# Narrow heads' scores as a pair, two engines on the queries' banks, and a rearranged start and end of a latent attention stage

## The chip, the core and the metric

The kernel runs on one core of a Trainium2 chip. The core has a matrix engine (TensorE, PE in the profile; its weight loads are a row of their own, PEld), a vector engine (VectorE, DVE), a scalar engine (ScalarE, ACT), a general engine (GpSimd, POOL) and a queue engine for transfers (SyncE, SP). Each engine works through its own instructions in order and waits for others through semaphores. Matmul results land in PSUM, which holds eight banks of 512 float32 numbers per partition; everything else stands in SBUF, which has 128 partitions. The metric is the device time of one execution in microseconds (us); lower is better.

## The reference

Two transformer layers run on x of shape (2, 1024, 256), float32. Each adds an attention and a feed-forward part to x, both computed from the same normalized x. The change lies in the attention of the second layer, a latent attention with 16 heads. The lines that matter:

```python
q = rmsnorm(hidden_states @ wq_a.T, q_a_ln_w) @ wq_b.T
q_nope, q_pe = (q[..., :NOPE], q[..., NOPE:])
ckv = hidden_states @ wkv_a.T
kv = rmsnorm(ckv[..., :KV_LORA], kv_a_ln_w)
k_pe = ckv[..., KV_LORA:][:, None, :, :]
q_pe = apply_rope(q_pe, cos, sin)
k_pe = apply_rope(k_pe, cos, sin)
q_abs = jnp.einsum('bhsd,hdc->bhsc', q_nope, q_absorb)
scores = (jnp.einsum('bhsc,btc->bhst', q_abs, kv) + jnp.einsum('bhsd,bxtd->bhst', q_pe, k_pe)) * SCALE
scores = jnp.where(causal, scores, jnp.finfo(scores.dtype).min)
attn = jax.nn.softmax(scores, axis=-1)
x = jnp.einsum('bhst,btc->bhsc', attn, kv)
x = jnp.einsum('bhsc,hdc->bhsd', x, out_absorb)
return x.transpose(0, 2, 1, 3).reshape(b, s, NH * VH) @ wo.T
```

Keys and values are the same 64 latent numbers per token, shared by all heads; a query has those 64 (the latent part) and 64 rotated ones. The mask is causal, so a block of 128 query tokens needs only the keys up to its own end.

## The kernel before

Everything up to 769 us of the span (the first layer, the second layer's feed-forward, keys, folded weights) is untouched. The stage of the change is the second layer's attention, from about 770 us to the end. Its order of work is written out by hand (`manual_schedule`): the engines take instructions in the order of the program text, and the framework adds the semaphore waits from the order in which tiles are written and read.

**Steps.** There are 16 steps: two batches, four pairs of query blocks (i, 7 - i), and two groups `g` of eight heads. The wide block i has 1024, 896, 768 or 640 keys, the narrow one 128, 256, 384 or 512. Each step has four cycles (c = 0 to 3); a cycle takes two heads of the wide block and two of the narrow one.

**Scores (`scores`, L1046 to L1069).** A head's scores are matmuls of up to 512 keys into a pair of PSUM banks (L1059; each float32 matmul shows as two passes in the profile), then DVE masks them, writes them negated to SBUF and takes the row's minimum (L1064, with a small read of the accumulator), then ACT takes the exponential and the row sum (L1067). A wide head takes a whole pair of banks. The two narrow heads share a pair, one bank each; the second stands in the program behind the first one's maximum and exponential. `turn_over` (L1073) transposes the weights in 32 by 32 blocks on DVE at the end of the cycle.

**Banks.** Pairs of banks (`pair`, tag "s") exist twice. Scores, projected queries, the transposed reciprocals and the output use them in turn. The other four banks hold the value products of one step (`ps_o`).

**What else a cycle holds.** While step s has its scores taken, the step before (`prev`) gets a quarter of its value products in each cycle (`product`, L1107: 72 small matmuls, 144 passes) and the step before that (`older`) is finished: `normalize` (L1117, DVE) at c = 0, `output` (L1130) at c = 1, `add` (L1142) at c = 2, and with it the transfer out for the second group. `inverse` (L1078 on DVE, L1081 on POOL) makes the reciprocals of the row sums of `prev` at c = 0, and `inverse_T` (L1092, and copies by ACT at L1098) transposes them at c = 3.

**Queries of the next step.** At c = 0 and c = 2 a block's queries are projected (`Query.project`, L994 and L1001): one bank holds the part to rotate, the other the latent part of both halves of the heads. In `rotate`, ACT copies the first bank to `t1` (L1018), then the latent parts (L1008, two copies of 64 partitions), then two halves of `t1`, swapped, to `t2` (L1022). POOL multiplies by cosine and sine (L1023, L1024) and adds into `qc` (L1028, four adds of 32 partitions). For the very first step the two projections and rotations stand ahead of all cycles; there DVE multiplies, DVE and POOL add, and both queries use the one `t1` and the one `t2`.

**The end.** After the last step with scores comes one pass of one cycle with all 36 blocks of value products of the last step in a row, then the output of the step before it, then the reciprocals; then a last pass normalizes, multiplies out, adds and stores.

Of the kernel before, what the change touches and what calls it, by code (L numbers as in the profile page):

```python
# [17 lines left out]
F32 = mybir.dt.float32  # L18
# [5 lines left out]
P = 128  # L24
# [4 lines left out]
SC = 512  # L29
# [17 lines left out]
def two_layers(ctx: ExitStack, tc: tile.TileContext, a: dict, out: bass.AP):  # L47
# [56 lines left out]
    with ExitStack() as scope:  # L104
# [233 lines left out]
        def scores(g, n, pair):  # L338
            iq, j = WEIGHTS[n]
            k, q = heads[g, 1], heads[g, 0]  # L340
            w = WIDTH[n]
            at = (4 * iq + 4) * P - w
            if (g, n) not in held:
                held[g, n] = l0t.tile([P, 4, SC], F32, tag="p", name="p", bufs=3)
            p = held[g, n]
            t = ps_pair()
            for c in pair:
                nc.tensor.matmul(  # L348
                    t[:, c % 2, :w], quad(k, c, D0 + 1)[:, j * P : (j + 1) * P],
                    quad(q, c, D0 + 1)[:, at : at + w],  # L350
                    start=True, stop=True, tile_position=(32 * c, 0),
                )

            def weights():
                nc.scalar.activation(p[:, pair[0] : pair[0] + 2, :w], t[:, :, :w], AF.Exp)  # L355
                if j >= 4 * iq:

                    nc.gpsimd.affine_select(  # L358
                        out=p[:, pair[0] : pair[0] + 2, :P], in_=p[:, pair[0] : pair[0] + 2, :P],
                        compare_op=ALU.is_ge, fill=0.0, base=0,  # L360
                        pattern=[[0, 2], [1, P]], channel_multiplier=-1,
                    )

            return weights
# [589 lines left out]
    with ExitStack() as scope:  # L954
# [8 lines left out]
        def pair(name):  # L963
            return ps.tile([P, 2, SC], F32, tag="s", name=f"ps_{name}", bufs=2)
# [6 lines left out]
        class Query:  # L971
# [33 lines left out]

            def latent(self):
                for hh in range(2):
                    nc.scalar.copy(  # L1008
                        self.qc[0:64, hh].rearrange("p r t -> p (r t)"),
                        self.lat[64 * hh : 64 * hh + 64],  # L1010
                    )

            def rotate(self, ahead=False):

                one, two = (nc.vector, nc.gpsimd) if ahead else (nc.gpsimd, nc.gpsimd)
                cos, sin = (t.unsqueeze(1).to_broadcast([P, QP, P]) for t in self.trig)
                t1 = att.tile([P, QP, P], F32, tag="t1", name="t1")
                nc.scalar.copy(t1.rearrange("p r t -> p (r t)"), self.pe)  # L1018
                self.latent()
                t2 = att.tile([P, QP, P], F32, tag="t2", name="t2")  # L1020
                for lo, hi in ((0, 64), (64, 0)):
                    nc.scalar.copy(t2[lo : lo + 64], t1[hi : hi + 64])  # L1022
                one.tensor_tensor(t1, t1, cos, ALU.mult)  # L1023
                one.tensor_tensor(t2, t2, sin, ALU.mult)  # L1024
                for hh in range(2):
                    for x in range(2):
                        at = 64 * x + 32 * hh
                        (one, two)[x].tensor_tensor(  # L1028
                            self.qc[64 + 32 * x : 96 + 32 * x, hh], t1[at : at + 32],
                            t2[at : at + 32], ALU.add,  # L1030
                        )
# [11 lines left out]
            s.p, s.q = {}, ready[b, i, g]  # L1043
            return s

        def scores(s, k, h):  # L1046

            w = P * (s.blocks[k] + 1)
            lo = 0
            if k == 0 or h % 2 == 0:  # L1050
                s.sc = pair("s").rearrange("p k c -> p (k c)")
                s.pp = att.tile([P, S], F32, tag="p", name="p", bufs=3)
            else:
                lo = SC
            sc, p = s.sc[:, lo : lo + w], s.pp[:, lo : lo + w]
            s.p[k, h] = p
            for n0 in range(0, w, SC):
                n1 = min(n0 + SC, w)
                nc.tensor.matmul(  # L1059
                    sc[:, n0:n1], s.q[k].qc[:, h // QP, h % QP, :],  # L1060
                    kT[:, s.b * S + n0 : s.b * S + n1], start=True, stop=True,
                )
            nmax = small.tile([P, 1], F32, tag="nmax", name="nmax")
            nc.vector.tensor_tensor_reduce(  # L1064
                p, sc, maskw[:, S - w :], -1.0, 3.0e38, ALU.add, ALU.min, nmax
            )
            nc.scalar.activation(  # L1067
                p, p, AF.Exp, bias=nmax, scale=-1.0, accum_out=s.rsum[:, k, h : h + 1]
            )  # L1069

        def turn_over(s, k, h):
            at = slice(0, s.nsb) if k == 0 else slice(s.nsb, NSB)
            nc.vector.transpose(s.pT[:, at, h, :], s.p[k, h])  # L1073

        def inverse(s):

            rinv = att.tile([P, 2, NH2], F32, tag="rinv", name="rinv", bufs=2)
            nc.vector.reciprocal(rinv, s.rsum)  # L1078
            s.rb = att.tile([P, 2, QP, 2, 64], F32, tag="rb", name="rb")
            for k in range(2):  # L1080
                nc.gpsimd.tensor_copy(  # L1081
                    s.rb[:, k],
                    rinv[:, k].rearrange("p (h r) -> p r h", h=2).unsqueeze(3).to_broadcast(
                        [P, QP, 2, 64]
                    ),
                )
# [27 lines left out]
        def normalize(s, k):  # L1114
            if k == 0:
                s.xT = att.tile([P, 2, QP, P], F32, tag="xT", name="xT")
            nc.vector.tensor_tensor(  # L1117
                s.xT[:, k].rearrange("p r (c y) -> p r c y", c=4),
                s.o[:, :, k * P : (k + 1) * P].rearrange("p c (r y) -> p r c y", r=QP),
                s.rT[:, k].rearrange("p (r c y) -> p r c y", r=QP, c=4), ALU.mult,  # L1120
            )
# [28 lines left out]
        with tc.manual_schedule():  # L1150
            steps = [(b, i, g) for b in range(B) for i in range(TB - 1, TB // 2 - 1, -1) for g in range(2)]
            ready = {}

            def ahead(step):

                b, i, g = step
                known = (b, i) == steps[0][:2]
                ready[step] = [
                    Query(b, t, g, k if known else None) for k, t in enumerate((i, TB - 1 - i))
                ]  # L1160
                return ready[step]

            for q in ahead(steps[0]):
                q.project()
                q.rotate(ahead=True)

            prev, older = None, None
            for at in range(len(steps) + 2):
                s = new_step(*steps[at]) if at < len(steps) else None
                nxt = ahead(steps[at + 1]) if at + 1 < len(steps) else ()  # L1170
                cycles = NCY if s is not None else 1
                for c in range(cycles):
                    heads = [] if s is None else [(k, 2 * c + h) for k in range(2) for h in range(2)]
                    if c == 0 and older is not None:
                        normalize(older, 0)
                        fetch_x(older)
                    if c == 2 and older is not None:
                        add(older)
                    for k, h in heads[:1]:
                        scores(s, k, h)  # L1180
                    if c == 0 and older is not None:
                        normalize(older, 1)
                    for k, h in heads[1:]:
                        scores(s, k, h)
                    if prev is not None:
                        for sb in range(c * NSB // cycles, (c + 1) * NSB // cycles):
                            product(prev, sb)
                    q = nxt[c // 2] if nxt and c % 2 == 0 else None
                    if q is not None:
                        q.project()  # L1190
                    if c == min(1, cycles - 1) and older is not None:
                        output(older)
                    if prev is not None:
                        if c == 0:
                            inverse(prev)
                        if c == cycles - 1:
                            inverse_T(prev)
                    for k, h in heads:
                        turn_over(s, k, h)
                    if q is not None:  # L1200
                        q.rotate()
                if s is None and older is not None:
                    add(older)
                older, prev = prev, s

# [66 lines left out]
```

## Time and profile before

| what | value |
|---|---|
| times of three runs, us | 1471.72, 1478.02, 1473.11 (median 1473.11) |
| the profiled execution | 1475.92 us, span 1474.2 us, mean granted TensorE clock 0.956 |
| busy in 811.4 to 1446.3 us of the span (634.9 us) | PE 556.2, DVE 374.6, ACT 302.3, POOL 237.5 us |
| granted clock there | 1.00 |
| idle before PE's score matmuls (L1059) from 778 us on | 84.3 us, of which 68.1 end with a maximum (nmax, L1064) |
| one value product run of a cycle (144 passes) | 2.32 us |

How to read the profile. A line of the timeline gives the start and the length in us, the engine, the line of the program, the operation, what is written and read, the shape, and how many instructions are merged; in brackets stands how long the engine was idle before and what ended that. A line of the waits gives who waited for whom, the total in us, how often, and the longest. A line of the windows gives the length of a stretch, then each engine's busy time and count, the granted clock as a share, the share of the DMA engines and their GB/s. Ends of matmuls are modelled, and consecutive matmuls overlap: the next starts before the last one's modelled end.

### The profile page before, as it was taken

The numbers are of one execution on the slowest core, as the hardware profiler recorded it, in microseconds if no ns is written. First come the engines' busy times: TensorE is split into PE (matmuls) and PEld (weight loads), VectorE is DVE, ScalarE is ACT, GpSimd is POOL, SyncE is SP. The second block draws the span as 40 slices with busy tenths as digits, with TensorE's granted clock in tenths as the row PEclk, the third lists the DMA queues.
The fourth block names the chain that finished last, engine by engine and source line by source line (L and its number), as shares of the span: only waits on it lengthen the run. The fifth ranks groups of instructions, "written<-read, shape, count | busy, mean of one in ns | idle before, by whom it ended". The sixth has DMA issues, their size and how long they took to land.

```text
span 1474.2 us, 36254 instructions
## 1 busy us (share of the span) xinstructions
PE 1317.6 (89%) x15614; PEld 781.1 (53%) x15614; DVE 770.3 (52%) x1893; ACT 671.6 (46%) x1250; POOL 460.4 (31%) x494
## 2 busy tenths in 40 slices
PE   6689999899999989998997888888888888888986
PEld 2233346264563543555774566565665656666655
DVE  3775544545456553124336656565556565655662
ACT  1224573453637546553315545445444454444441
POOL 2233333342414221003213444244334433443320
PEclk9659999899999999999997999999999999999999
DMA  4212301010101000001233000000000000000000
GB/s 179 74 31 56 101 8 23 0 23 1 22 1 22 23 1 18 15 1 54 59 95 58 5 17 6 24 10 23 10 12 17 6 27 6 24 9 15 11 17 10
DMA packets 61007, 41.09 MB, mean 28 GB/s; under 512 B 37648, under 2 KB 56848, under 8 KB 60592
## 3 DMA queue, kind: packets, MB, share of 16 engines
q1 hardware_dynamic: 60000, 35.51, 9.0%
q8 instruction: 122, 2.00, 0.6%
q0 software_dynamic: 416, 2.49, 0.4%
q10 hardware_dynamic: 432, 0.79, 0.2%
q14 instruction: 37, 0.30, 0.1%
HBM read 26.18 MB, written 10.49 MB: 25 GB/s over the span
## 4 chain that ended last, share of the span: by engine, by line
PE 77%; DVE 11%; ACT 5%; issue 4%; POOL 2%; DMA 1%; SPq 0%; ACTq 0%; DVEq 0%; POOLq 0%
PE ps_s L1059 12%; PE ps_m L307 11%; PE ps_o L1107 10%; DVE p L1064 6%; PE ps_m L558 5%; PE ps_o L373 5%; PE ps_m L461 4%; PE ps_m L430 4%; PE ps_t L1001 4%; PE ps_t L1130 4%; PE ps_m L228 4%; PE ps_t L994 2%; PE ps_m L573 2%; ACT qc L1008 2%; ACT t L1018 1%
## 5 line engine op out<-in xcount | busy, mean ns | idle before, releaser
L1059 PE MATMUL ps_s<-kT,qc 128*128 128x512 f32 (+3 forms) x768 | 290.7, 506 | 84.3 <-DVE nmax L1064 68.1
L1064 DVE CUSTOM_DVE_ANT_0 p<-ps_s,wpe 128x128 f32<-128x128 f32 (+7 forms) x256 | 189.7, 756 | 217.2 <-PE ps_s L1059 216.7
L1067 ACT ACTIVATE p<-p,nmax 128x128 f32<-128x128 f32 (+7 forms) x256 | 197.1, 770 | 187.4 <-DVE nmax L1064 186.1
L1059 PEld LDWEIGHTS ps_s<-kT,qc 128*128 128x128 f32 x768 | 129.8, 191 | 221.7 <-DVE nmax L1064 98.2
L355 ACT ACTIVATE p<-ps_s 128x1024 f32<-128x1024 f32 (+1 forms) x192 | 152.6, 808 | 167.1 <-PE ps_s L348 162.1
L307 PE MATMUL ps_m<-head,head 16*128 16x512 f32 (+3 forms) x672 | 193.7, 552 | 20.1 <-DVE nmx L318 14.0
L1073 DVE STREAM_TRANSPOSE pT<-p 128x128 f32<-128x128 f32 (+7 forms) x256 | 175.3, 742 | 0.0
L348 PE MATMUL ps_s<-head,head 17*128 17x512 f32 (+3 forms) x768 | 172.2, 553 | 0.0
L1028 POOL TENSOR_TENSOR qc<-t,t 32x512 f32<-32x512 f32 x124 | 158.8, 1280 | 34.9 <-issue 22.2
L1107 PE MATMUL ps_o<-pT,vrep 32*64 32x128 f32 x9216 | 152.1, 275 | 7.6 <-issue 5.3
L1107 PEld LDWEIGHTS ps_o<-pT,vrep 32*64 32x64 f32 x9216 | 135.5, 131 | 37.4 <-issue 35.9
L307 PEld LDWEIGHTS ps_m<-head,head 16*128 16x128 f32 x672 | 71.8, 189 | 119.7 <-DVE nmx L318 38.6
L1023 POOL TENSOR_TENSOR t<-t,cosq 128x512 f32<-128x512 f32 x28 | 35.7, 1274 | 293.9 <-issue 203.3
L358 POOL TENSOR_SCALAR_AFFINE_SELECT p<-p 128x256 f32<-128x256 f32 x128 | 51.5, 408 | 242.2 <-ACT p L355 241.0
L323 DVE TENSOR_REDUCE nmx<-ps_m 128x1 f32<-128x512 f32 x112 | 72.2, 686 | 44.0 <-PE ps_s L348 35.3
L558 PE MATMUL ps_m<-xnT,w 128*128 128x512 f32 x192 | 94.4, 620 | 0.0
L318 DVE CUSTOM_DVE_ANT_0 junk<-ps_m,maskz,nmx 128x512 f32<-128x512 f32 (+3 forms) x112 | 57.7, 548 | 59.2 <-PE ps_s L348 40.8
L1018 ACT COPY t<-ps_t 128x512 f32<-128x512 f32 x32 | 18.8, 586 | 146.5 <-PE ps_t L1001 126.0
L373 PE MATMUL ps_o<-p,v 128*32 128x512 f32 (+3 forms) x768 | 82.3, 501 | 0.0
L461 PEld LDWEIGHTS ps_m<-wpr,hT 128*128 128x128 f32 x512 | 62.3, 199 | 17.7 <-issue 6.6
L430 PE MATMUL ps_m<-xnT,wfc 128*128 128x512 f32 x128 | 68.6, 661 | 0.2
L461 PE MATMUL ps_m<-wpr,hT 128*128 128x128 f32 x512 | 68.5, 289 | 0.0
(175 smaller groups left out, 1786.7 us busy)
## 6 DMA issues: line engine op xcount, KB each, us to landing
rows<-proj SPq DMA_DIRECT2D x12, 512.0 KB, 2.6
stage<-rows SPq DMA_DIRECT2D x96, 64.0 KB, 3.1
w<-in_w SPq DMA_DIRECT2D x3, 768.0 KB, 4.7
x_sb<-in_x SPq DMA_DIRECT2D x4, 512.0 KB, 12.4
x<-x_sb SPq DMA_DIRECT2D x4, 512.0 KB, 3.2
fold_wo<-in_wo SPq DMA_DIRECT2D x8, 256.0 KB, 3.2
vrep<-kv SPq DMA_DIRECT2D x32, 64.0 KB, 2.1
xin<-x SPq DMA_DIRECT2D x16, 128.0 KB, 2.2
```

What stands on the lines that cost most here:

```text
L307: nc.tensor.matmul(t[:, :w], quad(q, c, D0)[:, i * P : (i + 1) * P], quad(k, c, D0)[:, k0 : k0 + w], start=True, stop=True, tile_position= ...
L348: nc.tensor.matmul(t[:, c % 2, :w], quad(k, c, D0 + 1)[:, j * P : (j + 1) * P], quad(q, c, D0 + 1)[:, at : at + w], start=True, stop=True, ...
L355: nc.scalar.activation(p[:, pair[0] : pair[0] + 2, :w], t[:, :, :w], AF.Exp)
L373: nc.tensor.matmul(quad(box["o"], c)[:, SC - w :], values[g][:, j, 32 * c : 32 * c + 32], p[:, c, :w], start=(j == 0), stop=(j == 4 * iq + ...
L461: nc.tensor.matmul(po[:, :P], f["h", hc // 2][:, hc % 2, t * P : (t + 1) * P], wpr[:, hc, cols], start=(hc == 0), stop=(hc == NH0 - 1),)
L558: nc.tensor.matmul(pw, w1t[f"w{i + 1}"][:, kc, hc * P : (hc + 1) * P], xnT1[n // 2][:, kc, (n % 2) * SC : (n % 2 + 1) * SC], start=(kc == ...
L1028: (one, two)[x].tensor_tensor(self.qc[64 + 32 * x : 96 + 32 * x, hh], t1[at : at + 32], t2[at : at + 32], ALU.add,)
L1059: nc.tensor.matmul(sc[:, n0:n1], s.q[k].qc[:, h // QP, h % QP, :], kT[:, s.b * S + n0 : s.b * S + n1], start=True, stop=True,)
L1064: nc.vector.tensor_tensor_reduce(p, sc, maskw[:, S - w :], -1.0, 3.0e38, ALU.add, ALU.min, nmax)
L1067: nc.scalar.activation(p, p, AF.Exp, bias=nmax, scale=-1.0, accum_out=s.rsum[:, k, h : h + 1])
L1073: nc.vector.transpose(s.pT[:, at, h, :], s.p[k, h])
L1107: nc.tensor.matmul(s.o[64 * hh : 64 * hh + 64, c, k * P : (k + 1) * P], vrep[32 * c : 32 * c + 32, s.b * 32 + sb, :], s.pT[32 * c : 32 * c ...
```

## The change

Four things move.

- `scores` takes a list of heads. For the narrow block it gets both heads of the cycle: their matmuls come first, then for each head the maximum and the exponential.
- In `rotate` the latent part is copied by DVE instead of ACT.
- The first step's two rotations get tiles of their own (two halves of a tile with the tag "p", of which there are three). The first is done by DVE alone; in the second POOL multiplies and adds the odd quarters, DVE adds the even ones. `rotate` takes the three engines as an argument.
- The pass after the last step has four cycles like the others: the value products come in quarters, the output of the step before stands after the second quarter, the transposed reciprocals after the third. `inverse` stands behind the first wide head of c = 0 instead of behind the projection.

```diff
             def latent(self):
                 for hh in range(2):
-                    nc.scalar.copy(
+                    nc.vector.tensor_copy(
                         self.qc[0:64, hh].rearrange("p r t -> p (r t)"),
                         self.lat[64 * hh : 64 * hh + 64],
                     )
...
-            def rotate(self, ahead=False):
-
-                one, two = (nc.vector, nc.gpsimd) if ahead else (nc.gpsimd, nc.gpsimd)
+            def rotate(self, engines=(nc.gpsimd, nc.gpsimd, nc.gpsimd), first=False):
+
+                one, even, odd = engines
...
-                t1 = att.tile([P, QP, P], F32, tag="t1", name="t1")
+                if first:
+                    t = att.tile([P, S], F32, tag="p", name="t12", bufs=3)
+                    t1, t2 = (
+                        t[:, SC * x : SC * x + SC].rearrange("p (r t) -> p r t", r=QP) for x in range(2)
+                    )
+                else:
+                    t1 = att.tile([P, QP, P], F32, tag="t1", name="t1")
+                    t2 = att.tile([P, QP, P], F32, tag="t2", name="t2")
...
-                        (one, two)[x].tensor_tensor(
+                        (even, odd)[x].tensor_tensor(
...
-        def scores(s, k, h):
+        def scores(s, k, hs):
...
+            sc = pair("s").rearrange("p k c -> p (k c)")
+            pp = att.tile([P, S], F32, tag="p", name="p", bufs=3)
+            for j, h in enumerate(hs):
+                for n0 in range(0, w, SC):
+                    n1 = min(n0 + SC, w)
+                    nc.tensor.matmul(
+                        sc[:, j * SC + n0 : j * SC + n1], s.q[k].qc[:, h // QP, h % QP, :],
+                        kT[:, s.b * S + n0 : s.b * S + n1], start=True, stop=True,
+                    )
+            for j, h in enumerate(hs):
+                p = s.p[k, h] = pp[:, j * SC : j * SC + w]
+                nmax = small.tile([P, 1], F32, tag="nmax", name="nmax")
+                nc.vector.tensor_tensor_reduce(
+                    p, sc[:, j * SC : j * SC + w], maskw[:, S - w :], -1.0, 3.0e38, ALU.add, ALU.min,
+                    nmax,
+                )
...
-            for q in ahead(steps[0]):
+            for k, q in enumerate(ahead(steps[0])):
                 q.project()
-                q.rotate(ahead=True)
+                v, p = nc.vector, nc.gpsimd
+                q.rotate((p, v, p) if k else (v, v, v), first=True)
...
-                cycles = NCY if s is not None else 1
-                for c in range(cycles):
-                    heads = [] if s is None else [(k, 2 * c + h) for k in range(2) for h in range(2)]
+                for c in range(NCY if prev is not None or s is not None else 1):
...
+                    h0, h1 = 2 * c, 2 * c + 1
+                    heads = [] if s is None else [(0, [h0]), (0, [h1]), (1, [h0, h1])]
+                    for k, hs in heads[:1]:
+                        scores(s, k, hs)
+                    if c == 0:
+                        if older is not None:
+                            normalize(older, 1)
+                        if prev is not None:
+                            inverse(prev)
+                    for k, hs in heads[1:]:
+                        scores(s, k, hs)
                     if prev is not None:
-                        for sb in range(c * NSB // cycles, (c + 1) * NSB // cycles):
+                        for sb in range(c * NSB // NCY, (c + 1) * NSB // NCY):
                             product(prev, sb)
...
-                    if c == min(1, cycles - 1) and older is not None:
+                    if c == (1 if prev is not None else 0) and older is not None:
                         output(older)
-                    if prev is not None:
-                        if c == 0:
-                            inverse(prev)
-                        if c == cycles - 1:
-                            inverse_T(prev)
+                    if prev is not None and c == (NCY - 1 if s is not None else 2):
+                        inverse_T(prev)
...
-                if s is None and older is not None:
+                if prev is None and older is not None:
                     add(older)
```

## The prediction

> **What bounds the kernel now.** I read the page first (busy shares, chain, groups), then the waits of the last stage alone (from 778 us on, where all edited code runs), then its timeline.
>
> ```profile
> PE 1317.6 (89%) x15614; PEld 781.1 (53%) x15614; DVE 770.3 (52%) x1893; ACT 671.6 (46%) x1250; POOL 460.4 (31%) x494
> ...
> PE 77%; DVE 11%; ACT 5%; issue 4%; POOL 2%; DMA 1%; SPq 0%; ACTq 0%; DVEq 0%; POOLq 0%
> ```
>
> ```profile
> PEld ps_s L1059 <- DVE nmax L1064: 98.2, 71, 1.6
> ...
> PE ps_s L1059 <- DVE nmax L1064: 68.1, 67, 2.6
> ...
> PE ps_s L1059 <- ACT qc L1008: 12.0, 24, 0.9
> ```
>
> ```profile
> 811.40:1446.30 634.90, 556.17 (x10637) 380.57 (x10644) 374.56 (x792) 302.26 (x663) 237.46 (x205) 1.00 0.05 14
> ```
>
> TensorE bounds the stage: 556 of 635 us busy at clock 1.00 (DVE 375, ACT 302, POOL 237), and its idle time is nearly all in front of score matmuls. Each line gives total, count and longest: 68.1 us end with a maximum (DVE), 12.0 with an ACT copy of the latent queries; the weight loads see the first wait from their own earlier start (98.2). One cycle from the timeline shows both:
>
> ```profile
> 1007.43 3.49 PE L1059 MATMUL ps_s<-kT,qc 128*128 128x512 f32 x10
> ...
> 1011.09 0.55 DVE L1064 CUSTOM_DVE_ANT_0 p<-ps_s,wpe 128x384 f32<-128x384 f32 x1
> ...
> 1011.71 0.91 PE L1059 MATMUL ps_s<-kT,qc 128*128 128x384 f32 x2 [0.79 <-DVE nmax L1064]
> ...
> 1012.55 2.32 PE L1107 MATMUL ps_o<-pT,vrep 32*64 32x128 f32 x144
> ...
> 1018.03 0.59 ACT L1018 COPY t<-ps_t 128x512 f32<-128x512 f32 x1 [4.07 <-PE ps_t L1001]
> ...
> 1018.52 1.17 ACT L1008 COPY qc<-ps_t 64x512 f32<-64x512 f32 x2
> ...
> 1019.74 2.20 PE L1059 MATMUL ps_s<-kT,qc 128*128 128x512 f32 x6 [0.51 <-ACT qc L1008]
> ```
>
> The ten passes at 1007.43 are both wide heads and the first narrow one. The second narrow head starts at 1011.71, 0.06 us after the first one's maximum ended (1011.65 with its accumulator read), though it writes the other half of the tile. After a projection (c = 0, 2) the next cycle's second wide head waits until ACT has emptied the projection's two banks: 1.96 us after the first wide head started at 1017.78.
>
> **Part 1, narrow scores in front of their maxima.** Both matmuls now stand ahead of any read of their tile, so the second follows the first. Removed: the 68.1 us, less 4.3 us (2.62, 0.84, 0.84) that belong to first narrow heads of the first two steps: 63.8 us in 64 cycles. A gap is counted from the modelled end of the matmul before, 0.165 us after the point at which the next could have started (0.49 us long, 0.32 apart at 384 columns): +10.6 us. The second pass behind a wait starts 0.105 us later than in an unbroken row: +6.7 us. Together 81.1 us: 1.38, 1.29, 1.03 and 0.95 us a cycle at narrow widths 128, 256, 384, 512, and 0.105 each. In the first step there are no value products behind the scores; there DVE sets the pace (a wide maximum 797.47, the next cycle's 804.47; its own work is 1.14x2 + 0.21x2 + 2.75 = 5.5 of these 7.0 us). Its four cycles hold 5.2 of the 81.1 us; I count 0.9 each (DVE's waits of 0.85 and 0.58, less what returns), 3.6. Sum 79.5 us; bounds 40 (rival 2) and 81.
>
> Is anything late next? Products now come 1.72 us (512 columns) to 0.43 us (128) after the first narrow start. In c = 0 they need the second normalization of the step two back, which reads their banks: at width 1024 it ends 3.76 us after the first wide start (1115.34 against 1111.58), the products would come at 3.87. Just covered. DVE per cycle at width 768: maxima 2.7, transposes 2.75, plus normalizations 1.4 in c = 0, latent copies 1.3 after a projection: at most 8.2 of PE's 9.3 us (10.35 from 1007.43 to 1017.78, less 1.06). The short cycle, c = 3, shrinks from 9.1 (to 1026.86) to 7.6 us against DVE's 5.5. POOL's rotation of the second query ends for the heads needed first 7.3 us after its projection (1.24 + 1.27 + two adds of 1.31, begun after ACT's copies at 2.1); they are read 10 us or more behind it (7.6 and two wide heads).
>
> **Part 2, latent copies on DVE.** 64 copies leave ACT (0.58 each), 64 come to DVE. Nearest row: DVE copies of 512 columns out of PSUM, 0.69; two PSUM reads in a row (1465.63) take 1.29. They start with ACT's copy of the other bank, 0.25 us after the next first wide start, and end at 1.55 instead of 1.91: the second wide head at 1.60 instead of 1.96. It wants 1.72, 1.50, 1.29, 1.075 at widths 1024, 896, 768, 640. Gains: 8 waits of about 0.27, then 22 of 0.36: 10 us. Bounds: all thirty gone, 16.6 us; or DVE slowed as its adds beside POOL are (0.68 alone, 1.65 at worst): the pair takes 3.3, minus 1.64 x 30 = minus 49 us. I take 10, since the copies are nearest to the PSUM reads. Behind them on DVE wait the next cycle's maxima (0.06 us later at 768, 0.24 at 640; nobody waits for that: the first narrow head comes later still). ACT's shorter queue lets exponentials and POOL start up to 1.17 us earlier, off the path.
>
> **Part 3, first rotation.**
>
> ```profile
> 779.29 2.42 PE L1059 MATMUL ps_s<-kT,qc 128*128 128x512 f32 x4 [3.27 <-POOL qc L1028]
> ...
> 780.94 0.59 ACT L1018 COPY t<-ps_t 128x512 f32<-128x512 f32 x1 [4.93 <-POOL qc L1028]
> ...
> 787.67 1.22 DVE L1064 CUSTOM_DVE_ANT_0 p<-ps_s,wpe 128x1024 f32<-128x1024 f32 x1
> ```
>
> The second query's copy waited 4.93 us for the shared t1, and DVE's first maximum for that rotation. With own tiles: ACT's copies of the first end at 775.0; DVE does two products and four adds at 0.69 (776.4, 779.1), its first head pair at 777.8. The second query is copied at 776.1 to 778.0; POOL multiplies until 780.55, DVE copies its latents until 780.4; adds beside POOL, 2.35 for two, end at 782.9. First maximum 782.9: 4.8 us. The clock was 0.5 from 780.7 to 794.4 and from 808.0 to 811.4: the two projections there took 4.4 us each, later ones 2.9. Bounds: 2 (the second query's adds at 1.65 each, and ACT and DVE in each other's way) and 8 (those two projections at full clock as well, 3.0). The Trainium skill, "TensorE: Matmul & The Clock Gate", Part 1, has the clock halve after an idle window of about 3.4 us and return after a busy one. By that the shorter gaps (about 1.8, 0.8, 1.1) would keep it full, 3 us more; I leave them out of the sum, since a gap of 1.07 us (at 454.95) also stands before 6.8 us of half clock from 456.4 on.
>
> **Part 4, the end.**
>
> ```profile
> 1446.02 7.43 PE L1107 MATMUL ps_o<-pT,vrep 32*64 32x128 f32 x360 [2.09 <-DVE xT L1117]
> ...
> 1455.12 2.10 PE L1107 MATMUL ps_o<-pT,vrep 32*64 32x128 f32 x128 [1.67 <-issue]
> ...
> 1466.47 3.69 PE L1130 MATMUL ps_t<-wvo,xT 128*128 128x256 f32 x16 [1.49 <-DVE xT L1117]
> ```
>
> The last run of 576 passes takes 14.4 us where four of 144 take 9.3; its stalls (1.67, 1.66) come 128 passes apart, 3.75 us from start to start: instructions arrive in portions. The output (3.3 us) and the reciprocals' transposes (1.0) now stand amid the run, while portions arrive, and with them DVE's addition of the other group (0.69, no DMA). Products end near 1461.0 instead of 1460.4, then 1.0 us for a normalization: the last output starts at 1462.0 instead of 1466.5, 4.5 us. Bounds 0.4 (the bubble alone) and 6. The Trainium skill, "Runtime: NRT & Kernel Launch", Instruction fetch mechanics, calls such fetches mostly hidden; by that the gain would be 0.4. The stalls' even spacing speaks against it here. Elsewhere such stalls cost 2.7 us in the stage now; tighter cycles may add 2 (bounds 0, 10).
>
> **Part 5, inverse earlier.** The reciprocal (0.25) and POOL's copies (1.17) only move; their reader stands at c = 3. Nothing.
>
> **Sum.** 79.5 + 10 + 4.8 + 4.5 - 2 = 96.8 us. The profiled execution took 1475.9 (span 1474.2, 1.7 around it), 2.8 above the median 1473.1; so 1379 for it, 1376 for the median. I say 1377.
>
> **Rivals.** (1) The copies on DVE are slowed beside POOL: 1.64 lost where 0.33 was won, 30 times, 59 us dearer: 1435. For: DVE's adds at 785.28. Against: maxima out of PSUM keep 0.96 with POOL running (1021.34) and without (1008.92). (2) The first narrow head becomes late: it starts 0.15 us after its bank's wide maximum ends (1009.88, 1010.03). If DVE ran 0.75 later in each cycle, 64 x 0.6 = 38 us would return: 1414. Against: DVE has an idle 3.4 us before the first maximum (1019.27). (3) The change doesn't do what it says: the second narrow matmul waits for something else that ends with that maximum. Then parts 2 to 4 stay: 1456. For: the halves are separate banks. Against: a wide head's two halves, issued together, show no wait. (4) Slower: the copies, queued in order, hold up the maxima behind them; that decides once a pair takes over 4.5 us (1.3 + 97/30), 2.3 a copy; at 2.6 the thirty pairs cost 117 us more: 1493. No PSUM read here of 512 columns takes over 0.75.
>
> **Chances.** Forecast 0.74 (own range 1362 to 1395: part 1 down to 65, part 2 to 16.6, part 3 to 8, the stalls up to 10), rival (1) 0.06, (2) 0.10, (3) 0.06, (4) 0.04. A measurement can tell about 0.5%, 7 us. Faster 0.94, within 0.02 (rival 3 with the low ends of the rest), slower 0.04. The range takes in the forecast and rival (2): 1362 to 1414.
>
> **What would show it.** Waits of L1059 on nmax below 8 us; L1059's waits on the latent copies about 3 us and by DVE; the first maximum near 783; two output groups apart at the end; PE over 95% busy in the stage. Wrong would be: the same gap under another releaser, DVE copies well over 0.7 us, or a clock below 1.00 in the denser stage.

## The result, and the profile after

| | before | after |
|---|---|---|
| median of four runs, us | 1472.41 (1470.4 to 1478.02) | 1403.72 (1401.44 to 1405.06) |
| ratio, 95% interval | | 0.9526 [0.9496, 0.9556] |
| profiled execution, span, us | 1475.92, 1474.2 | 1405.06, 1403.4 |
| first query's projection to first maximum, us | 17.86 | 15.02 |
| first maximum to the transposed reciprocals of step 14, us | 655.17 | 594.67 |
| from there to the end, us | 31.38 | 26.90 |

The kernel is 68.7 us faster by the medians, 70.9 by the two spans. The forecast was 96.8. From the page of the kernel after: busy shares, the PE instruction queue, the chain that ended last, and the groups of the score matmuls and of the latent copies.

```profile
PE 1292.5 (92%) x15614; PEld 778.2 (55%) x15614; DVE 810.4 (58%) x1957; ACT 635.7 (45%) x1186; POOL 460.2 (33%) x494
...
q8 instruction: 122, 2.00, 0.6%
...
PE 82%; DVE 8%; issue 4%; ACT 4%; POOL 1%; DMA 1%; SPq 0%; DVEq 0%; ACTq 0%; POOLq 0%
...
L1061 PE MATMUL ps_s<-kT,qc 128*128 128x512 f32 (+3 forms) x768 | 270.6, 493 | 34.5 <-DVE qc L1008 26.6
...
L1008 DVE COPY qc<-ps_t 64x512 f32<-64x512 f32 x64 | 44.0, 688 | 80.4 <-ACT t L1025 75.9
```

The 64 copies have gone from ACT's count to DVE's. The idle time before the score matmuls fell from 84.3 to 34.5 us, but most of what is left now ends with a DVE copy. The waits of the stage (total, count, longest, us) and the window of its middle:

```profile
DVE qc L1008 <- ACT t L1025: 75.9, 30, 4.1
...
PE ps_s L1061 <- DVE qc L1008: 26.6, 31, 1.9
...
PE ps_o L1112 <- issue: 7.8, 11, 1.2
...
PE ps_s L1061 <- DVE nmax L1068: 5.8, 6, 2.6
```

```profile
788.00:1376.00 588.00, 551.50 (x10651) 389.47 (x10654) 418.54 (x870) 275.98 (x621) 245.13 (x210) 1.00 0.06 16
```

The waits on maxima fell from 68.1 to 5.8 us. The waits on the latent copies rose from 12.0 to 26.6, and each copy pair itself was released by ACT's copy (75.9 us in 30 is idle time of DVE, not of PE). PE is busy for 551.5 of 588 us, 94%. One cycle of the timeline after (start, length, engine, line):

```profile
980.60 4.13 PE L1061 MATMUL ps_s<-kT,qc 128*128 128x512 f32 x12
...
984.66 1.88 PE L1112 MATMUL ps_o<-pT,vrep 32*64 32x128 f32 x112
...
986.87 0.70 PE L1112 MATMUL ps_o<-pT,vrep 32*64 32x128 f32 x32 [0.33 <-issue]
...
990.48 1.46 PE L1061 MATMUL ps_s<-kT,qc 128*128 128x512 f32 x4
...
990.73 0.59 ACT L1025 COPY t<-ps_t 128x512 f32<-128x512 f32 x1 [3.99 <-PE ps_t L1001]
...
991.35 1.39 DVE L1008 COPY qc<-ps_t 64x512 f32<-64x512 f32 x2 [2.86 <-ACT t L1025]
...
992.88 2.82 PE L1061 MATMUL ps_s<-kT,qc 128*128 128x512 f32 x8 [0.95 <-DVE qc L1008]
...
999.01 1.07 ACT L1103 COPY rT<-ps_t 128x512 f32<-128x512 f32 x2 [1.33 <-PE ps_t L1097]
...
999.63 0.69 DVE L1122 TENSOR_TENSOR xT<-ps_o,rT 128x512 f32<-128x512 f32 x1 [0.18 <-ACT rT L1103]
```

All twelve passes of a cycle now run in one row (980.60): no gap in front of the second narrow head. After a projection the second wide head starts 2.40 us behind the first (992.88 against 990.48); before it was 1.96. DVE's pair begins only when ACT's copy of the other bank has ended (991.35), not beside it.

Counted from start to start of the matmul passes, each beyond its regular step, the two profiles differ like this (us, positive is gained):

| place | before | after | gained | forecast |
|---|---|---|---|---|
| second narrow head, both passes | 81.3 | 0.1 | 81.2 | 81.1 |
| given back in the first step | 0.35 | 3.27 | -2.9 | -1.6 |
| second wide head behind a projection, 30 times | 16.57 | 29.63 | -13.1 | 10 |
| stalls inside product runs, middle | 3.35 (5) | 9.58 (11) | -6.2 | -2 |
| start, to the first maximum | 17.86 | 15.02 | 2.85 | 4.8 |
| the end | 31.38 | 26.90 | 4.5 | 4.5 |
| ahead of the stage, code that is not edited | 769.80 | 766.76 | 3.0 | 0 |

They sum to 69.4 of 70.9; 1.5 are left over in small steps. The last row is not the change's, which leaves about 68 us for the change: in other profiles of this study the first projection starts at 761.9 to 770.0 us.

### The profile page after: what moved, and what is told of

It reads as the page before. It is cut to its first block, busy times and chain, and to the rows that moved or that the text cites. A ratio compares the mean times of both kernels' runs of the same rounds, so it can differ in the third digit from the quotient of the medians.

```text
span 1403.4 us, 36314 instructions
## 1 busy us (share of the span) xinstructions
PE 1292.5 (92%) x15614; PEld 778.2 (55%) x15614; DVE 810.4 (58%) x1957; ACT 635.7 (45%) x1186; POOL 460.2 (33%) x494
## 4 chain that ended last, share of the span: by engine, by line
PE 82%; DVE 8%; issue 4%; ACT 4%; POOL 1%; DMA 1%; SPq 0%; DVEq 0%; ACTq 0%; POOLq 0%
PE ps_s L1061 14%; PE ps_m L307 11%; PE ps_o L1112 10%; PE ps_m L558 6%; PE ps_o L373 5%; PE ps_m L461 5%; PE ps_t L1001 4%; PE ps_m L430 4%; PE ps_t L1135 4%; PE ps_m L228 4%; PE ps_m L573 3%; PE ps_t L994 2%; DVE qc L1008 2%; ACT t L1025 1%; PE ps_s L307 1%
## 5 line engine op out<-in xcount | busy, mean ns | idle before, releaser
L1061 PE MATMUL ps_s<-kT,qc 128*128 128x512 f32 (+3 forms) x768 | 270.6, 493 | 34.5 <-DVE qc L1008 26.6
L1068 DVE CUSTOM_DVE_ANT_0 p<-ps_s,wpe 128x128 f32<-128x128 f32 (+7 forms) x256 | 185.0, 752 | 60.5 <-PE ps_s L1061 59.5
L1034 POOL TENSOR_TENSOR qc<-t,t 32x512 f32<-32x512 f32 x120 | 152.6, 1271 | 8.1
L1008 DVE COPY qc<-ps_t 64x512 f32<-64x512 f32 x64 | 44.0, 688 | 80.4 <-ACT t L1025 75.9
L461 PEld LDWEIGHTS ps_m<-wpr,hT 128*128 128x128 f32 x512 | 61.2, 196 | 17.1 <-issue 6.6
L318 DVE CUSTOM_DVE_ANT_0 junk<-ps_m,maskz 128x512 f32<-128x512 f32 (+3 forms) x112 | 50.5, 488 | 34.3 <-PE ps_s L348 31.6
```

What stands on the lines that cost most here:

```text
L461: nc.tensor.matmul(po[:, :P], f["h", hc // 2][:, hc % 2, t * P : (t + 1) * P], wpr[:, hc, cols], start=(hc == 0), stop=(hc == NH0 - 1),)
L1034: (even, odd)[x].tensor_tensor(self.qc[64 + 32 * x : 96 + 32 * x, hh], t1[at : at + 32], t2[at : at + 32], ALU.add,)
L1061: nc.tensor.matmul(sc[:, j * SC + n0 : j * SC + n1], s.q[k].qc[:, h // QP, h % QP, :], kT[:, s.b * S + n0 : s.b * S + n1], start=True, sto ...
L1068: nc.vector.tensor_tensor_reduce(p, sc[:, j * SC : j * SC + w], maskw[:, S - w :], -1.0, 3.0e38, ALU.add, ALU.min, nmax,)
```

## The experiments

**1 and 2. Each of the two large parts alone.** To the kernel before, `part1_only` adds only the narrow pair:

```diff
-        def scores(s, k, h):
+        def scores(s, k, hs):
...
-                    heads = [] if s is None else [(k, 2 * c + h) for k in range(2) for h in range(2)]
+                    heads = [] if s is None else [(0, [h0]), (0, [h1]), (1, [h0, h1])]
```

and `part2_only` only the other engine for the latent copies:

```diff
-                    nc.scalar.copy(
+                    nc.vector.tensor_copy(
                         self.qc[0:64, hh].rearrange("p r t -> p (r t)"),
```

> Only the narrow heads' scores as a pair; everything else as before. Serial theory (in the changed kernel the DVE copies wait for ACT's copy of the other bank of the same tile, and that, not the pairing, lengthened the second wide head's wait from 0.28-0.88 to 0.68-1.33 us): the pairing gives 81 us less 3 in the first step and 3 to 6 in instruction stalls, so 1396 to 1400, and the second wide heads behind a projection still wait 0.28 to 0.88 us. Rival (denser cycles alone lengthen that wait): it is 0.7 to 1.3 us here too, and the time is 1405 or more.

> Only the latent copies on DVE; everything else as before. Serial theory: the pair of copies starts 0.6 us after ACT's copy and ends 0.44 us later than ACT alone did; 30 projections, 13 us slower, 1485. The prediction's part 2 (both engines at once): 10 us faster, 1462. Rival (denser cycles): no serial start, 1462 to 1472.

Measured: `part1_only` 1395.14 us, ratio 0.9489 [0.9468, 0.9511]; `part2_only` 1482.72 us, ratio 1.0088 [1.0064, 1.0113], 0.9% slower: a small difference, but its interval lies above 1. Waits of the first, then of the second:

```profile
PE ps_s L1055 <- ACT qc L1008: 11.8, 24, 0.8
...
PE ps_s L1055 <- DVE nmax L1062: 6.1, 7, 2.6
```

```profile
PE ps_s L1059 <- DVE nmax L1064: 69.0, 67, 3.0
PE ps_s L1059 <- DVE qc L1008: 26.6, 31, 1.8
```

By the medians the narrow pair alone is worth more than the whole change (the intervals overlap by 0.0015). With the copies still on ACT, the delay of the second wide head stays at 16.54 us in the thirty places although the cycles are denser, so density is not what makes it longer. With the copies on DVE and the old narrow heads it is 29.66 us. By widths 1024, 896, 768 and 640 one delay is 0.28, 0.46, 0.67 and 0.88 us with ACT, and 0.69, 0.90, 1.12 and 1.33 with DVE, 0.41 to 0.45 more each time.

**3. The change with the copies given back to ACT** (`lat_act`, the second diff above in reverse, on the kernel after).

> The changed kernel with the latent copies back on ACT. Serial theory: 13 us faster than the changed kernel, 1390 to 1391, waits of the second wide head back at 0.28 to 0.88 us. Rival (denser cycles): no gain or a loss of up to 10, 1404 to 1414.

Measured: 1393.4 us (1389.63 to 1395.54), ratio 0.9468 [0.9439, 0.9497]; the delays are 16.18 us in all. Its waits:

```profile
PE ps_s L1061 <- ACT qc L1008: 10.7, 22, 0.7
PE ps_o L1112 <- issue: 8.5, 12, 1.3
PE ps_s L1061 <- DVE nmax L1068: 6.8, 7, 3.4
```

That is 2.4 us above the expected 1391. Part 2 costs the kernel 10.3 us by the medians (8.5 by the ratios, each against its own runs of the kernel before; the intervals of the two ratios just touch); 13.4 of delays come back in the profile. The product stalls (issue) stay, so they come with the denser cycles and not with the copies (`part1_only` has them too, 10.7 us in 12).

**4 and 5. The wait covered.** `amid_act` is `lat_act` with the projection put behind five of the nine product blocks of its cycle; the other four come behind the projection, in front of the next scores, while the copies run. `amid_dve` does the same with the copies on DVE.

```diff
-                        for sb in range(c * NSB // NCY, (c + 1) * NSB // NCY):
+                        cut = c * NSB // NCY + 5
+                        for sb in range(c * NSB // NCY, cut):
                             product(prev, sb)
...
+                    if prev is not None:
+                        for sb in range(cut, (c + 1) * NSB // NCY):
+                            product(prev, sb)
```

> As lat_act, and the next step's projection stands behind five of a cycle's nine blocks of value products instead of behind all nine, so that four blocks (about 1 us of PE) and a wide head lie between a projection and the next user of its banks. Serial theory, with the copies ending 1.7 us behind the projection: all 30 waits of the second wide head vanish, 16.6 us and 0.1 for each second pass, 1371 to 1374, unless the projection now waits for the second wide maximum (up to 0.3 us in 16 cycles, then 1376). If those waits hang on something else than the copies' end, 1390.

> As amid_act, but with the latent copies on DVE as in the changed kernel. Serial theory: the copies still end 0.44 us later than with ACT alone, but four blocks of products (about 1 us) and a wide head (1.08 to 1.72 us) now cover them, so nothing is lost: 1372 to 1376, the waits of the second wide head under 0.2 us. Rival (DVE itself is short of time and the copies hold up the maxima): 1380 or more, with PE waiting for nmax.

Measured: `amid_act` 1373.71 us (1372.47 to 1380.42), ratio 0.9352 [0.9322, 0.9381]; `amid_dve` 1376.52 (1375.81 to 1381.63), ratio 0.9365 [0.9329, 0.94], 0.5 above its expected range. Waits and window of `amid_act`:

```profile
PE ps_s L1061 <- DVE nmax L1068: 6.8, 7, 3.4
...
PE ps_o L1112 <- issue: 0.9, 2, 0.6
```

```profile
783.00:1343.00 560.00, 555.18 (x10673) 394.04 (x10671) 377.62 (x811) 307.92 (x682) 244.82 (x210) 1.00 0.06 17
```

The delays behind projections fall to 0.46 us with ACT and 1.35 with DVE. PE is busy for 555.2 of 560 us, 99%. Once four product blocks stand in front of the wait, the two engines are 2.8 us apart, with overlapping intervals: DVE's later copies seem to cost something only where PE waits for them. The cut also takes 10.2 us of stalls out of the kernel (11.55 to 1.36); the last section says what they are.

**6 and 7. Bank or tile?** In every kernel so far the projection's two halves are two banks of one PSUM tile. Two kernels that leave out the fourth row group's value products, and so free one bank, differ only in where the latent half lies: `three_shared` keeps it in the shared tile, `three_own` gives it a tile of its own.

```diff
-                self.pe, self.lat = t[:, 0], t[:, 1]
+                self.pe = t[:, 0]
+                self.lat = ps.tile([P, SC], F32, tag="l", name="ps_l")
```

> The changed kernel without the fourth row group's value products (a quarter of the keys is left out of the values, the output is not the reference's), so that the products take three banks; the queries' two parts still share a tile. Any theory: DVE's copy starts 0.6 us after ACT's, waits of the second wide head 0.68 to 1.33 us as in the changed kernel; within 10 us of 1404.

> As three_shared (the same quarter left out), with the latent part in a tile of its own in the bank left over. Serial theory, if the shared tile is what makes DVE wait: DVE's copy starts within 0.1 us of ACT's, and the second wide head, which now needs only ACT's copy, waits less than 0.1 us: 30 waits of 0.99 on average gone, about 30 us (27 to 34) faster than three_shared. Rival (DVE and ACT cannot read PSUM at the same time, whatever the tile): DVE still starts 0.6 us later; the second wide head is freed all the same.

Measured, one time each: 1384.04 and 1364.21 us. The middle takes 577.53 and 550.28 us, 27.3 less; 5.9 us of that are given back in the untouched code ahead of the stage, which varies. The timelines, shared first:

```profile
980.43 0.59 ACT L1025 COPY t<-ps_t 128x512 f32<-128x512 f32 x1 [3.30 <-PE ps_t L1001]
...
981.05 1.39 DVE L1008 COPY qc<-ps_t 64x512 f32<-64x512 f32 x2 [2.17 <-ACT t L1025]
...
982.59 2.82 PE L1061 MATMUL ps_s<-kT,qc 128*128 128x512 f32 x8 [0.95 <-DVE qc L1008]
```

```profile
975.30 0.59 ACT L1026 COPY t<-ps_t 128x512 f32<-128x512 f32 x1 [2.40 <-PE ps_t L1002]
...
975.94 4.27 PE L1062 MATMUL ps_s<-kT,qc 128*128 128x512 f32 x12
...
976.21 1.39 DVE L1009 COPY qc<-ps_l 64x512 f32<-64x512 f32 x2 [1.57 <-PE ps_l L1002]
```

With a shared tile DVE is released by ACT's copy, 0.62 us after that began and 0.98 after the projection's last pass started. With its own tile it is released by its own matmuls, 0.38 after that pass started, and the twelve score passes run without a gap; the delays fall from 29.61 to 0.02 us, also because the second wide head there waits for ACT's copy alone. The semaphores in the traces say the same: with the shared tile DVE's copy waits for the one that ACT's copy raises (number 116 here), with its own tile for the one that the matmuls raise (117). So the wait hangs on the tile, by an order that stands in the program, not on the engine or its speed. Two expectations were missed: `three_shared` was 20 us faster than `after`, not within 10 (a quarter of the product instructions is gone, and only one stall is left), and in `three_own` ACT's copy started 0.9 us before DVE's, because its half of the projection also ends earlier. That the two copies would run at the same time is therefore not shown by this pair. The timeline after shows the two engines reading PSUM at the same time elsewhere: ACT's copies of `rT` (999.01 to 1000.08) overlap DVE's normalization (999.63 to 1000.32), which reads another PSUM tile.

The Trainium skill, "PSUM — Partial Sum Buffer", Specifications (TRN2), lets ScalarE and VectorE read PSUM in parallel so long as they are not in the same bank. The overlap at 999.63 agrees, with 0.69 us for the normalization as elsewhere; the page does not speak of the order by tiles that the program keeps here.

**8 to 10. Further in the same direction.** `best` is `amid_act` with the output and the transposed reciprocals also standing amid the product run of their cycles, the second first-step rotation wholly on POOL, and the first step's latent copies behind ACT's swapped ones. `amid_start` has only the two edits at the start. `amid_some` is `amid_start` with the cut only in steps of width 896 and below.

```diff
-                q.rotate((p, v, p) if k else (v, v, v), first=True)
+                q.rotate((p, p, p) if k else (v, v, v), first=True)
...
-                self.latent()
+                if not first:
+                    self.latent()
...
+                if first:
+                    self.latent()
```

Of `best` alone, and then of `amid_some`:

```diff
                         inverse_T(prev)
+                    if prev is not None:
+                        for sb in range(cut, (c + 1) * NSB // NCY):
+                            product(prev, sb)
```

```diff
-                        cut = c * NSB // NCY + 5
+                        cut = (c * NSB // NCY + 5) if s is not None and s.blocks[0] < TB - 1 else (c + 1) * NSB // NCY
```

> amid_act with three more moves: output and transposed reciprocals amid the products too, the first step's second rotation wholly on POOL, and the latent copies of the first step behind the swapped copies. The start then leaves DVE free for the first two maxima: first narrow heads about 11 us after the first projection instead of 16, 4 to 5 us; the waits for the transposed reciprocals (0.25 us in 4 cycles) go. 1367 to 1371. If the start is bound by the half clock instead, no gain: 1373.

> amid_act with only the two moves at the start that best had as well (second rotation wholly on POOL, latent copies of the first step behind the swapped ones); output and transposed reciprocals stand behind all products again. If best lost its 12 us to cutting the other two cycles' product runs (0.34 us a cut, 29 cuts), this has amid_act's middle, 565 to 567 us, and best's start, 10.4 us from the first projection to the first maximum: 1368 to 1370. If best lost them to its start (POOL busy with the second rotation while the first step needs it), the middle is 575 or more: 1378.

> As amid_start, but the product runs are cut only in steps with wide blocks of 896 keys or fewer, where the wait that a cut removes (0.46 to 0.88 us and 0.1 for the next pass) is longer than its own price of 0.34; at 1024 keys the wait was 0.23 to 0.28. Gain of a cut there 0, so within 2 us of amid_start; if cuts also save the instruction stalls there (five of lat_act's ten stood in those steps), 4 us slower.

| kernel | median, us | ratio | start | middle | end |
|---|---|---|---|---|---|
| `amid_act` | 1373.71 | 0.9352 [0.9322, 0.9381] | 14.95 | 565.56 | 27.63 |
| `best` | 1381.24 | 0.9392 [0.9359, 0.9425] | 10.38 | 577.47 | 27.45 |
| `amid_start` | 1370.47 | 0.9304 [0.9272, 0.9336] | 10.39 | 567.39 | 28.43 |
| `amid_some` | 1374.60 | 0.9339 [0.9307, 0.9372] | 10.39 | 570.94 | 27.10 |

The start edits are worth 4.6 us in the profiles (14.95 to 10.39). `best` was expected to be faster than `amid_act` and lost 10 us in the middle against `amid_start`. PE's own timelines, `amid_start` and then `best`, show where:

```profile
984.21 2.32 PE L1115 MATMUL ps_o<-pT,vrep 32*64 32x128 f32 x144
986.46 1.09 PE L1100 MATMUL ps_t<-ident,rb 128*128 128x128 f32 x8
987.39 3.10 PE L1064 MATMUL ps_s<-kT,qc 128*128 128x512 f32 x9
```

```profile
987.45 1.43 PE L1115 MATMUL ps_o<-pT,vrep 32*64 32x128 f32 x80
988.81 1.09 PE L1100 MATMUL ps_t<-ident,rb 128*128 128x128 f32 x8
989.84 1.21 PE L1115 MATMUL ps_o<-pT,vrep 32*64 32x128 f32 x64
990.97 1.24 PE L1064 MATMUL ps_s<-kT,qc 128*128 128x512 f32 x3
```

From start to start, the uncut sequence takes 3.18 us (987.39 - 984.21), the cut one 3.52 (990.97 - 987.45); at the output, the other place, it is 5.81 and 6.15. One cut of a product run costs 0.34 us, and `best` has 29 more of them: 10 us, for no wait that they could cover. Behind a projection a cut buys 0.54 us (16.18 us of delays over 30) and the stalls besides. `amid_some` asked whether to leave it out where the delay is smallest, 0.28 us at width 1024: it got 6 stalls of 5.58 us instead of 3 of 2.47, and was 4 us slower by the medians, 3.6 in the middle, with intervals that overlap. Four of its five stalls in the middle stand in the uncut steps of width 1024, so the cut seems to pay there through the stalls. Of the kernels that compute everything, `amid_start` has the lowest median of the study, 33 us under the change.

## Why the prediction was right or wrong

The direction was right, and 1403.72 lies inside 1362 to 1414, but above the likeliest case's own 1362 to 1395. It lies in the wider range only because that took in rival (2), which did not occur: that much is luck. Of the 96.8 us, 23.1 failed in one step.

- **Part 1, right.** 78.3 us net against 79.5. The removed delays are 81.2 against 81.1; the first step gives back 2.9 instead of 1.6. `part1_only` shows it alone.
- **Part 2, wrong.** The failed step is "They start with ACT's copy of the other bank". They start with its end: 0.62 us later, and the pair takes 1.39 us, so it ends 2.01 us after ACT's copy began. Two copies in a row on ACT (1.17 us, the first 0.49 behind the start of ACT's other copy) ended after 1.66. With the start of PE's next pass, 0.14 us behind a DVE copy and 0.05 behind an ACT copy, the second wide head comes 0.44 us later. Minus 13.1 where plus 10 stood. The rest of the step held: a copy took 0.688 us against 0.69 assumed, so DVE was not slowed. Bounds of minus 49 to 16.6 contained it, but through a slow DVE and not through an order. The hint stood in the same profile: a narrow head waited for a maximum that read the other bank of its tile, which the prediction itself remarked on ("though it writes the other half of the tile"), and part 2 then assumed that two readers of one tile are free of each other.
- **Instruction stalls, under-sized.** 6.2 us against 2, within the bounds of 0 to 10.
- **Part 3, mis-sized.** 2.85 us against 4.8, within 2 to 8. The first maximum came 15.02 us behind the first projection; the forecast, 782.9, was 13.1 behind it. Of the 1.9 us missing, 1.0 came with DVE's first four adds (3.77 us where 2.76 stood). DVE's latent copies behind them ended at 778.50 and its last two adds began at once, 1.0 us later than forecast; POOL's two products had grown as well (1.50 and 1.71, forecast 1.24 and 1.27), but ended at 778.20. The other 0.9 came with these last two adds (3.22 against 2.35). In the single records of the traces before and after, each of the five adds that DVE began while POOL was at work took 1.55 to 1.66 us and ended 0.54 to 0.55 us after POOL's instruction, and the other five took 0.68: here DVE's add waits for POOL's instruction to end. The prediction took the last two adds at 2.35, a pair of which only one is long; its bound of 2 us had both at 1.65. The timeline after, at the first rotations (start, length, engine, line):

```profile
773.31 3.77 DVE L1034 TENSOR_TENSOR qc<-t 32x512 f32<-32x512 f32 x4
...
775.03 1.50 POOL L1029 TENSOR_TENSOR t<-t,wpe 128x512 f32<-128x512 f32 x1 [22.55 <-DMA vrep<-kv]
...
776.49 1.71 POOL L1030 TENSOR_TENSOR t<-t,wpe 128x512 f32<-128x512 f32 x1
777.11 1.39 DVE L1008 COPY qc<-ps_t 64x512 f32<-64x512 f32 x2
778.28 2.93 POOL L1034 TENSOR_TENSOR qc<-t 32x512 f32<-32x512 f32 x2
778.53 3.22 DVE L1034 TENSOR_TENSOR qc<-t 32x512 f32<-32x512 f32 x2
...
781.78 1.23 DVE L1068 CUSTOM_DVE_ANT_0 p<-ps_s,wpe 128x1024 f32<-128x1024 f32 x1
```

- **The clock.** TensorE's granted clock was at half for 3.4 us after the first scores (784.3 to 787.8) instead of 17.1 us in two stretches. No gain from it is seen: from the first maximum to the start of the fourth projection it is 19.8 us before, 18.0 after, and also 18.0 in `part1_only`, whose clock was at half from 772.6 to 786.3, 6.5 us into that stretch. These 1.8 are what the narrow heads alone give there (5.2 us in the first step's four cycles less the 2.9 given back, three of the four cycles: 1.7). The Trainium skill, "TensorE: Matmul & The Clock Gate", Part 1, ties the halving to idle windows of about 3.4 us. Here gaps of 1.81, 1.90 and 2.56 us, none of that length, stood before a half-rate stretch. In `lat_act` gaps of 3.06 and 3.38 us stood before one that was no longer (3.4 us), so the runs do not show that the shorter gaps are what left fewer of them.
- **Part 4, right.** 4.5 us, and the mechanism too: the products stand around the first of two output groups, and only one stall is left of three.

The end of the timeline after:

```profile
1384.21 1.14 PE L1112 MATMUL ps_o<-pT,vrep 32*64 32x128 f32 x56 [1.03 <-issue]
...
1385.28 3.72 PE L1135 MATMUL ps_t<-wvo,xT 128*128 128x256 f32 x16
...
1395.58 3.72 PE L1135 MATMUL ps_t<-wvo,xT 128*128 128x256 f32 x16 [0.85 <-DVE xT L1122]
```

- **The rivals.** All four fall: (1) the copies kept 0.688 us (0.68 and 0.69 also at 777.11, beside POOL's product), (2) the waits on maxima are six of 5.8 us, (3) the pair does run as one, (4) a pair of copies takes 1.39 us, far from 4.5. The miss came from a case that was not on the list: the copy is ordered behind the other engine's.
- **What would show it.** Maxima below 8 us: 5.8. First maximum near 783: 781.78, but the stage started 3.0 us earlier, so counted from there it came 1.9 us late. Output groups apart: yes. PE over 95%: 94. Waits on latent copies about 3 us: 26.6, and this line names the failure.

## What to carry to other kernels

Before handing half of a PSUM tile's reads to a second engine, give that half a tile of its own; two engines on one tile run one behind the other here, and the second engine brought only a hand-over and, in this case, slower copies (0.69 against 0.58 us). Where an engine must wait for a copy, four product blocks put in front of the wait were worth more than a faster copy (20 us against 10, though part of the 20 are the instruction stalls that went with them). But count the price of each cut, and cut only where a wait or an instruction stall is covered.

## What the hardware showed

PE's instructions arrive in transfers of 16 KB (122 packets, 2.00 MB in all, for 15614 matmul passes and as many weight loads), each 256 instructions, which is 128 product passes with their weight loads. In the kernels before and after, all product stalls ended 2.2 to 2.9 us after such a transfer began, and no two transfers began closer than 3.4 us (3.2 in `amid_act`). A row of products uses 256 instructions up in about 2.0 us (2.25 for 144 passes), so it would run dry unless slower matmuls stand in between. That is inferred from these figures; it fits that denser cycles brought stalls (5 to 11 in the middle) and that a cut run took them away. The Trainium skill, "Runtime: NRT & Kernel Launch", Instruction fetch mechanics, calls the crossing of a 16 KiB boundary mostly hidden; the sizes agree, but the stalls in these two kernels are 0.3 to 1.9 us each, and up to 9.6 us in the middle of a kernel.

A stall and what precedes it, in the timeline after: 119 passes, then 1.22 us of nothing.

```profile
813.37 2.00 PE L1112 MATMUL ps_o<-pT,vrep 32*64 32x128 f32 x119
816.60 0.67 PE L1112 MATMUL ps_o<-pT,vrep 32*64 32x128 f32 x25 [1.22 <-issue]
```
